# Layer 0's expert blocks 12 to 59: rows turned four at a time by VectorE's square transposes and 16 SBUF transfers, with a lead of eight fetches

## The chip, the cores and the metric

The kernel runs on one core of one Trainium2 chip. The time is that of one execution on the device, in microseconds (us); a comparison uses the median of several runs. A profile is one further execution recorded by the hardware profiler, and takes somewhat longer than the runs without it. PE is TensorE, PEld its weight loads, DVE is VectorE, ACT is ScalarE, POOL is GpSimd, SP is SyncE, whose queue issues most plain DMAs. "L1698" is line 1698 of the kernel before.

## What is computed

Two layers of a transformer-like network on x of shape (4, 1024, 256), each an attention-like part and a mixture of experts, with a layer norm, a modulation and a gate around each. The change concerns the experts of layer 0:

```python
def _L0_ffn_ref(input_emb, W1, b1, W2, b2, Wr, br):
    logits = jnp.einsum('bsd,de->bse', input_emb, Wr) + br
    route_w = jax.nn.softmax(logits, axis=-1)
    _, topk_idx = jax.lax.top_k(route_w, TOP_K)            # 2 of 8 experts
    mask = jax.nn.one_hot(topk_idx, E, dtype=route_w.dtype).sum(-2)
    routed = route_w * mask
    routed = routed / routed.sum(axis=-1, keepdims=True)
    h = jax.nn.relu(jnp.einsum('bsd,edh->ebsh', input_emb, W1) + b1[:, None, None, :])
    expert_out = jnp.einsum('ebsh,ehd->ebsd', h, W2) + b2[:, None, None, :]
    return jnp.einsum('bse,ebsd->bsd', routed, expert_out)
# in reference():
h = _layernorm(x, axis=-1) * (1 + cb) + sb
x = x + gb * _L0_ffn_ref(h, L0_ffn_W1, L0_ffn_b1, L0_ffn_W2, L0_ffn_b2, L0_ffn_Wr, L0_ffn_br)
```

Each expert is a 256 to 1024 to 256 perceptron in fp32. 4096 tokens with two experts each give 8192 pairs of a token and an expert.

## The kernel before

The pairs are sorted by expert into blocks of 128 rows that share one expert, at most 71 blocks. `turning` is 60: blocks 0 to 59 are written out by a hand-ordered loop (L1776 to L1800), and blocks 60 to 67 are placed by a planner together with the start of layer 1 (`late_block`, L1806); the last three run only if the routing needs them. Within `tc.manual_schedule` each engine, SP too, executes its instructions in the order in which the program lists them.

For one block j the work is this.

- `g0.reach` (L746; VectorE, two instructions at L752), `g0.look` (L761; TensorE, two matmuls at L765) and `g0.find` (L774; VectorE) work out which 128 rows of the token table belong to the block. In the loop this is done for block j + 3.
- `g0.fetch` (L791) lets POOL gather these rows, 258 words each (256 features and two that say where the result goes), with an indirect DMA (the helper's line is L347). In the loop it is done for block j + 2, into one of four buffers `xgbuf`.
- `weights_in` and `weights_out` (L1686, L1689) gather W1 (1 MB with its bias) and W2 of the block's expert, double buffered; where the expert is that of two blocks before, the indices point beyond the table and nothing is moved.
- `turn_rows` (L1675) turns the 128 x 256 rows into features on partitions with two TensorE transposes (L1678) into PSUM, and `rows_turned` (L1681) copies them to SBUF on VectorE (L1683).
- `aimed` / `g0.aim` (L1737, L799) computes where the block's results are to be written.
- `hidden` (L1692) is 16 products of W1 with the turned rows, each two matmul instructions (L1698), and `rectified` (L1707) adds the bias and applies the ReLU on ACT (L1710).
- `values` (L1717) is 8 products with W2, again two instructions each (L1721), and `biased` (L1730) adds the second bias on VectorE (L1732); `kept` (L1740) lets POOL write the rows to HBM with a scatter (L812).

Iteration j of the loop lists, for TensorE: hidden of block j, the transposes of block j + 1, the count of block j + 3, values of block j - 1. For VectorE: reach of j + 3, the copy of the turned rows and the address of j + 1, find of j + 3, the bias add of j - 1. For POOL: W1 of j + 1, the scatter of j - 2, W2 of j, the rows of j + 2. `once` (L1765) adds work that belongs to later stages; from iteration 8 to 23 it lists one load of 512 KB each on SP (L1774: the weights and modulations of layer 1).

`early` (L1452) is a pool for tiles of the stage that follows (the combination of the experts' results and layer 1's first norm: `yg1`, `h1`, `hT1` and small ones). W1's rows are laid out on the host so that row p of the gathered tile holds features p and 128 + p, one after the other (L2528).

Of the kernel before, what the change touches and what calls it, by code (L numbers as in the profile page):

```python
# [8 lines left out]
F32 = mybir.dt.float32  # L9
F16 = mybir.dt.float16  # L10
I32 = mybir.dt.int32
# [8 lines left out]
P = 128  # L20
B, S, D = 4, 1024, 256
NC = S // P
KD = D // P
E = 8
H = 1024
KH = H // P
# [6 lines left out]
ROUTER = 64  # L33
STRIP = 32
AHEAD = 3
DX = D + 2
W1ROW = KD * H + KH
W2ROW = KH * D + D
# [101 lines left out]
def adaln_d2_kernel(  # L140
# [20 lines left out]
    nc = tc.nc  # L161
# [8 lines left out]
    ps_m = ctx.enter_context(tc.tile_pool(name="ps_m", bufs=3, space=PSUM))  # L170
# [79 lines left out]
    xgbuf = [pw.tile([P, DX], F32, name=f"xg_{i}") for i in range(4)]  # L250
# [108 lines left out]
    class Pairs:  # L359
# [386 lines left out]
        def reach(self, scratch, j):  # L746

            reached = scratch.tile(
                [P, self.halves, P], F16, tag="g_reached", name="g_reached", bufs=3
            )  # L750
            for h in range(self.halves):
                nc.vector.tensor_scalar(  # L752
                    reached[: self.K, h, :],
                    count16[: self.K],
                    self.limit[: self.K, h, j : j + 1],
                    None,
                    ALU.is_ge,
                )
            return reached
# [35 lines left out]
        def aim(self, scratch, xg, j):  # L795


            dest = scratch.tile([P, 1], I32, tag="g_dest", name="g_dest", bufs=8)
            nc.vector.scalar_tensor_tensor(  # L799
                dest,  # L800
                xg[:, D : D + 1],
                self.code[:, j : j + 1],
                xg[:, D + 1 : D + 2],
                ALU.not_equal,
                ALU.add,
            )
            return dest
# [566 lines left out]
    for piece in range(3):  # L1374
        ps = plan.slot("p2")
        m = loaded
# [72 lines left out]
    mods1 = [l1.tile([P, B, D], F32, name=f"mod{i}") for i in range(6)]  # L1449
    groups = [Pairs(l1, l1, "ga", 4 * B), Pairs(l1, l1, "gb", 3 * B)]  # L1450
    mod_rows1 = dram.tile([B, 6, D], F32, name="mod_rows1")
    early = ctx.enter_context(tc.tile_pool(name="early", bufs=1))  # L1452
    poolF = tc.tile_pool(name="poolF", bufs=2, side="right")
    work = poolF.__enter__()
    y0 = dram.tile([2 * B * S, D], F32, name="y0")
    groups_of["g0"], values_of["g0"] = g0, y0

# [23 lines left out]
    RINGS = tuple(room1)  # L1481
    SP = "SP"
    made = {}
    home = {"yg1": early, "h1": early, "hT1": early, "tiny": early}

    def buf(kind, shape):
        return (home[kind] if kind in home else late).tile(
# [187 lines left out]
    def turn_rows(j):  # L1675
        pt = psum(ps_m, [P, KD, P], "pm_x")
        for k in range(KD):
            nc.tensor.transpose(pt[:, k, :], xgbuf[j % 4][:, k * P : (k + 1) * P], ident)  # L1678
        return pt

    def rows_turned(pt):  # L1681
        xT = work.tile([P, KD, P], F32, tag="xT", name="xT", bufs=3)
        nc.vector.tensor_copy(xT, pt)  # L1683
        return xT

    def weights_in(j):  # L1686
        gather(w1buf[j % 2], W1, g0.wrow[:, j : j + 1], E * P - 1)
# [4 lines left out]
    def hidden(j, xT, m4):  # L1692
        w1 = w1buf[j % 2]
        p1 = psum(ps_1, [P, 4, P], "p1_h")
        for i in range(4):
            m = 4 * m4 + i
            for k in range(KD):
                nc.tensor.matmul(  # L1698
                    p1[:, i, :],
                    lhsT=w1[:, k * H + m * P : k * H + (m + 1) * P],  # L1700
                    rhs=xT[:, k, :],
                    start=(k == 0),
                    stop=(k == KD - 1),
                )
        return p1
# [11 lines left out]
    def values(j, hid):  # L1717
        w2 = w2buf[j % 2]
        p2 = psum(ps_2, [P, D], "p2_y")
        for m in range(KH):  # L1720
            nc.tensor.matmul(  # L1721
                p2,
                lhsT=hid[:, m, :],
                rhs=w2[:, m * D : (m + 1) * D],
                start=(m == 0),
                stop=(m == KH - 1),
            )
        return p2

    def biased(j, p2):  # L1730
        y = work.tile([P, D], F32, tag="y", name="y", bufs=3)
        nc.vector.tensor_tensor(y, p2, w2buf[j % 2][:, KH * D :], ALU.add)  # L1732
        return y

    dests, ys0 = {}, {}

    def aimed(j):  # L1737
        dests[j] = g0.aim(work, xgbuf[j % 4], j)
# [35 lines left out]
            nc.sync.dma_start(*loads[j - 8])  # L1774

    with tc.manual_schedule(engines=ORDERED | {EngineType.SP}):  # L1776
        for j in range(2):
            g0.fetch(xgbuf[j], h_rows, j)
        xT, hid = rows_turned(turn_rows(0)), None
        aimed(0)  # L1780
        for j in range(turning):

            weights_in(j + 1)
            if j > 1:
                kept(j - 2)
            if j:
                weights_out(j)
            g0.fetch(xgbuf[(j + 2) % 4], h_rows, j + 2)
            reached = g0.reach(work, j + AHEAD)
            new = new_hidden()  # L1790
            for m4 in range(2):
                rectified(j, new, hidden(j, xT, m4), m4)

            xT = rows_turned(turn_rows(j + 1))
            aimed(j + 1)
            g0.find(work, g0.look(ps_m, reached), j + AHEAD)
            if j:
                ys0[j - 1] = biased(j - 1, values(j - 1, hid))
            hid = new
            once(j)  # L1800


    plan = Plan(rings=RINGS, **room1)
    of_block = {}

# [762 lines left out]
```

## Time and profile before

| what | value |
|---|---|
| median of three runs (range) | 1121.61 us (1121.43 to 1122.06) |
| the profiled execution | 1141.97 us |
| its span, first to last instruction | 1140.2 us |
| granted TensorE clock, mean | 0.986 |
| blocks 0 to 67 of layer 0's experts, first and last L1698 | 115.0 to 615.1 us of the span |
| L1678, transposes of the rows | 136 instructions, 26.1 us busy |
| L1698, hidden products | 2176 instructions, 254.7 us busy |
| L1721, values products | 1088 instructions, 249.0 us busy |
| L765, counts in this stage | 136 instructions, 19.2 us busy |
| L1683, copies of the turned rows (DVE) | 68 instructions, 28.8 us busy |
| L347, gathers of weights (POOL) | 134 instructions, 135.1 us busy |

A group of the profile gives line, engine, operation, what it writes and reads with the shapes, how often, then busy time, the mean duration of one in ns, the engine's idle time just before the group's instructions and what ended most of it. A line of the timeline gives start and length in us, engine, line, operation and how many instructions were merged, and, in brackets, an idle time before it and what ended it. A line of a window gives its limits, its length, and for PE, PEld, DVE, ACT and POOL the busy time and the number of instructions; then the granted clock, the DMA engines' mean busy share and GB/s.

### The profile page before, as it was taken

Reading aid. Unit: us, or ns where it says so; the run is one execution under the profiler, and the core shown is the slowest. Engines: PE = TensorE matmul, PEld = TensorE weight load, DVE = VectorE, ACT = ScalarE, POOL = GpSimd, SP = SyncE. Lnnn points to the kernel's source line nnn. Section 1 sums busy time; section 2 is a strip of 40 time slices with the busy share of each in tenths; the row PEclk is TensorE's granted clock in tenths of the full one; section 3 lists DMA queues with packets and bytes.
Section 4 is the critical chain, followed back from the end, with each engine's and each line's share of the span. In section 5 each row is a group of like instructions: output and inputs, shape, how many; then the busy total and the mean of one; then the engine's idle time right before and its main releaser. Section 6 shows DMA issues by size and latency. Waiting matters only on the chain. (4 is left out here: it accounts for less than half of the span.)

```text
span 1140.2 us, 18501 instructions
## 1 busy us (share of the span) xinstructions
PE 1086.3 (95%) x6238; PEld 847.0 (74%) x6238; DVE 592.0 (52%) x2308; ACT 428.6 (38%) x1164; POOL 422.5 (37%) x483
## 2 busy tenths in 40 slices
PE   8998999999999999999999999999999999899883
PEld 5894999999999999999988466566576575547641
DVE  7787232222222222222274788975776445888456
ACT  5976333322333323233343343432434235333421
POOL 1000455555555555555543011010044233616452
PEclk8999999999999999999999999999999999999996
DMA  9414549242422415151260312100024223323532
GB/s 321 174 31 103 191 156 302 100 153 75 154 78 75 150 39 192 33 193 40 70 223 27 96 34 83 39 10 19 19 62 129 75 82 103 102 88 107 155 118 93
DMA packets 77693, 122.38 MB, mean 107 GB/s; under 512 B 27340, under 2 KB 57301, under 8 KB 72990
## 3 DMA queue, kind: packets, MB, share of 16 engines
q0 software_dynamic: 31872, 69.68, 19.5%
q1 hardware_dynamic: 44622, 49.92, 13.3%
q10 hardware_dynamic: 1104, 1.58, 0.4%
q8 instruction: 52, 0.85, 0.3%
q14 instruction: 43, 0.35, 0.1%
HBM read 205.25 MB, written 30.22 MB: 207 GB/s over the span
## 5 line engine op out<-in xcount | busy, mean ns | idle before, releaser
L1710 ACT ACTIVATE hid<-p_h,w 128x128 f32<-128x128 f32 x544 | 154.8, 368 | 323.5 <-issue 251.9
L1698 PEld LDWEIGHTS p_h<-xT,w 128*128 128x128 f32 x2176 | 253.2, 192 | 7.2 <-DVE xT L1683 1.9
L1698 PE MATMUL p_h<-xT,w 128*128 128x128 f32 x2176 | 254.7, 275 | 3.1 <-DVE xT L1683 2.7
L1721 PE MATMUL p_y<-w,hid 128*128 128x256 f32 x1088 | 249.0, 382 | 0.2 <-issue 0.2
L2007 PE MATMUL p_u<-hT,a 128*128 128x512 f32 x512 | 232.0, 596 | 2.9 <-ACT hf L2019 1.4
L1721 PEld LDWEIGHTS p_y<-w,hid 128*128 128x128 f32 x1088 | 201.6, 190 | 25.1 <-DMA w<-in_W,g_wrow 0.4
L2007 PEld LDWEIGHTS p_u<-hT,a 128*128 128x128 f32 x512 | 93.5, 190 | 100.5 <-issue 89.7
L347 POOL DMA_INDIRECT w<-in_W,g_wrow x134 | 135.1, 1008 | 77.4 <-ACT hid L1710 46.7
L1683 DVE COPY xT<-pm_x 128x256 f32<-128x256 f32 x68 | 28.8, 424 | 187.0 <-PE pm_x L1678 134.4
L812 POOL DMA_INDIRECT y<-y,g_dest x68 | 69.5, 1022 | 143.5 <-DVE g_reached L752 108.4
L2055 PE MATMUL p_f<-a,hf 128*128 128x256 f32 x512 | 116.7, 380 | 2.0 <-DVE step L2096 1.0
L1732 DVE TENSOR_TENSOR y<-p_y,w 128x256 f32<-128x256 f32 x68 | 28.9, 425 | 166.9 <-PE p_y L1721 160.7
L2055 PEld LDWEIGHTS p_f<-a,hf 128*128 128x128 f32 x512 | 95.9, 190 | 20.8 <-issue 5.9
L347 POOL DMA_INDIRECT xg<-h_rows,g_row x68 | 66.7, 980 | 120.4 <-DVE g_row L787 98.9
L2103 POOL TENSOR_TENSOR x_sb<-x_sb,step 128x256 f32<-128x256 f32 x32 | 24.9, 778 | 205.8 <-DVE step L2096 153.6
L2315 PE MATMUL p_e<-ew,xT 128*128 x280 | 71.5, 386 | 0.8 <-ACT y L2325 0.8
L2019 ACT ACTIVATE hf<-p_u,decay 128x512 f32<-128x512 f32 x56 | 38.2, 685 | 74.9 <-PE p_u L2007 63.5
L347 POOL DMA_INDIRECT xg<-ga_rows,ga_row x39 | 37.3, 956 | 54.1 <-DVE g_hits L778 19.3
L2315 PEld LDWEIGHTS p_e<-ew,xT 128*128 128x128 f32 x280 | 49.0, 190 | 11.0 <-issue 3.8
L2023 DVE SCALAR_TENSOR_TENSOR hf<-p_u,decay,hf 128x512 f32<-128x512 f32 x56 | 41.9, 748 | 25.7 <-PE p_u L2007 14.3
L1618 DVE TENSOR_TENSOR h<-h,mod 128x256 f32<-128x256 f32 x128 | 51.6, 425 | 6.8 <-ACT h L1608 4.1
L2325 ACT COPY y<-p_e 128x256 f32<-128x256 f32 x70 | 26.1, 373 | 51.4 <-PE p_e L2315 19.2
(371 smaller groups left out, 1259.1 us busy)
## 6 DMA issues: line engine op xcount, KB each, us to landing
yg<-y SPq DMA_DIRECT2D x32, 256.0 KB
ga_y<-y SPq DMA_DIRECT2D x39, 128.0 KB
x_sb<-in_x SPq DMA_DIRECT2D x8, 512.0 KB
h_rows<-xn SPq DMA_DIRECT2D x8, 512.0 KB
gb_y<-y SPq DMA_DIRECT2D x31, 128.0 KB
out_x<-x_sb SPq DMA_DIRECT2D x7, 512.0 KB
a<-in_fw SPq DMA_DIRECT2D x6, 512.0 KB
mod<-mod_rows SPq DMA_DIRECT2D x6, 512.0 KB
```

The costliest lines, as they stand in the source:

```text
L347: return nc.gpsimd.indirect_dma_start(out=dst, out_offset=None, in_=table, in_offset=bass.IndirectOffsetOnAxis(ap=index, axis=0), bounds_c ...
L812: nc.gpsimd.indirect_dma_start(out=table, out_offset=bass.IndirectOffsetOnAxis(ap=dest, axis=0), in_=y, in_offset=None, bounds_check=2 * s ...
L1618: nc.vector.tensor_tensor(h, h, mods1[(sc, sh)[i]][:, b, :], (ALU.mult, ALU.add)[i])
L1698: nc.tensor.matmul(p1[:, i, :], lhsT=w1[:, k * H + m * P : k * H + (m + 1) * P], rhs=xT[:, k, :], start=(k == 0), stop=(k == KD - 1),)
L1710: nc.scalar.activation(hid[:, m, :], p1[:, i, :], AF.Relu, bias=w1buf[j % 2][:, KD * H + m : KD * H + m + 1],)
L1721: nc.tensor.matmul(p2, lhsT=hid[:, m, :], rhs=w2[:, m * D : (m + 1) * D], start=(m == 0), stop=(m == KH - 1),)
L1732: nc.vector.tensor_tensor(y, p2, w2buf[j % 2][:, KH * D :], ALU.add)
L2007: nc.tensor.matmul(pu, lhsT=a[:, k, m * P : (m + 1) * P], rhs=made["n1", c, "hT"][:, k, :, :], start=(k == 0), stop=(k == KD - 1),)
L2019: nc.scalar.activation(made[key, m], made[key, m, 0], AF.Silu, scale=decays[c])
L2023: nc.vector.scalar_tensor_tensor(h, made[key, m, 1], decays[c], h, ALU.mult, ALU.mult)
L2055: nc.tensor.matmul(made[key, "p2", b], lhsT=made[key, m][:, b * P : (b + 1) * P], rhs=a1[:, m, :], start=(m == 0), stop=(m == KH - 1),)
L2315: nc.tensor.matmul(made[key, "p2"], lhsT=made[key, "xT"][:, k, :], rhs=ew_flat[:, bass.ds(made[key, "at"] + k * D, D)], start=(k == 0), st ...
```

## The change

Blocks 12 to 59 form twelve groups of four ("quads"). Their rows are gathered into two buffers that hold four blocks each. At the end of iteration j = 8, 12, ..., 52, behind the bias add, `quad_turned` turns the rows of blocks j + 4 to j + 7: for each of the two halves k of the features (every second feature, from k on) one VectorE instruction transposes all 32 x 32 squares of the four blocks, 512 columns on 128 partitions, into `square`. The squares then lie on the wrong partitions, and 16 DMAs from SP's queue, one for each pair of source and destination group of 32 partitions, move them, 1 KB per partition, into the tile `xTq`. The four addresses (`g0.aim`) follow on VectorE. TensorE's transposes and VectorE's copies from PSUM are left out for these 48 blocks; blocks 0 to 11 and 60 on keep them, but read every second feature too, and W1's rows are laid out accordingly on the host (row p holds features 2p and 2p + 1).

`hidden` now reads a half of a quad's block as four runs of 32 words, 1 KB apart. For the longer lead, rows are searched ten blocks ahead and fetched eight blocks ahead: iterations 2 to 8 search two blocks each and 4 to 9 fetch two each; from iteration 53 on nothing is searched and from 54 on nothing is fetched in the loop. The buffers for searches and addresses grow from 3 to 5 and from 8 to 16. The pool `early` is opened only after the loop, on the memory that the quads had.

```diff
--- before.py
+++ after.py
@@ -33,6 +33,8 @@
 ROUTER = 64
 STRIP = 32
 AHEAD = 3
+QUAD = 4
+SQ = 32
 DX = D + 2
 W1ROW = KD * H + KH
 W2ROW = KH * D + D
@@ -746,7 +748,7 @@
         def reach(self, scratch, j):
 
             reached = scratch.tile(
-                [P, self.halves, P], F16, tag="g_reached", name="g_reached", bufs=3
+                [P, self.halves, P], F16, tag="g_reached", name="g_reached", bufs=5
             )
             for h in range(self.halves):
                 nc.vector.tensor_scalar(
@@ -795,7 +797,7 @@
         def aim(self, scratch, xg, j):
 
 
-            dest = scratch.tile([P, 1], I32, tag="g_dest", name="g_dest", bufs=8)
+            dest = scratch.tile([P, 1], I32, tag="g_dest", name="g_dest", bufs=16)
             nc.vector.scalar_tensor_tensor(
                 dest,
                 xg[:, D : D + 1],
@@ -1449,9 +1451,11 @@
     mods1 = [l1.tile([P, B, D], F32, name=f"mod{i}") for i in range(6)]
     groups = [Pairs(l1, l1, "ga", 4 * B), Pairs(l1, l1, "gb", 3 * B)]
     mod_rows1 = dram.tile([B, 6, D], F32, name="mod_rows1")
-    early = ctx.enter_context(tc.tile_pool(name="early", bufs=1))
+    poolQ = tc.tile_pool(name="poolQ", bufs=2)
+    quads = poolQ.__enter__()
     poolF = tc.tile_pool(name="poolF", bufs=2, side="right")
     work = poolF.__enter__()
+    xgquad = [quads.tile([P, QUAD, DX], F32, name=f"xq_{i}", bufs=1) for i in range(2)]
     y0 = dram.tile([2 * B * S, D], F32, name="y0")
     groups_of["g0"], values_of["g0"] = g0, y0
 
@@ -1481,7 +1485,7 @@
     RINGS = tuple(room1)
     SP = "SP"
     made = {}
-    home = {"yg1": early, "h1": early, "hT1": early, "tiny": early}
+    home = {}
 
     def buf(kind, shape):
         return (home[kind] if kind in home else late).tile(
@@ -1675,13 +1679,40 @@
     def turn_rows(j):
         pt = psum(ps_m, [P, KD, P], "pm_x")
         for k in range(KD):
-            nc.tensor.transpose(pt[:, k, :], xgbuf[j % 4][:, k * P : (k + 1) * P], ident)
+            nc.tensor.transpose(pt[:, k, :], xgbuf[j % 4][:, k:D:KD], ident)
         return pt
 
     def rows_turned(pt):
         xT = work.tile([P, KD, P], F32, tag="xT", name="xT", bufs=3)
         nc.vector.tensor_copy(xT, pt)
-        return xT
+        return [xT[:, k, :] for k in range(KD)]
+
+    def in_quads(j):
+        return 3 * QUAD <= j < turning
+
+    def rows_of_block(j):
+        if in_quads(j):
+            return xgquad[j // QUAD % 2][:, j % QUAD, :]
+        return xgbuf[j % 4]
+
+    def quad_turned(j):
+
+        rows = xgquad[j // QUAD % 2]
+        square = quads.tile([P, P // SQ, KD, QUAD, SQ], F32, tag="square", name="square", bufs=1)
+        for k in range(KD):
+            nc.vector.transpose(
+                square[:, :, k, :, :].rearrange("p m b s -> p b m s"),
+                rows[:, :, k:D:KD].rearrange("p b (m f) -> p b m f", f=SQ),
+            )
+        xT = quads.tile([P, P // SQ, KD, QUAD, SQ], F32, tag="xTq", name="xTq")
+        for q in range(P // SQ):
+            for m in range(P // SQ):
+                nc.sync.dma_start(
+                    xT[m * SQ : (m + 1) * SQ, q, :, :, :], square[q * SQ : (q + 1) * SQ, m, :, :, :]
+                )
+        for b in range(QUAD):
+            turned_quads[j + b] = [xT[:, :, k, b, :] for k in range(KD)]
+            dests[j + b] = g0.aim(work, rows[:, b, :], j + b)
 
     def weights_in(j):
         gather(w1buf[j % 2], W1, g0.wrow[:, j : j + 1], E * P - 1)
@@ -1698,7 +1729,7 @@
                 nc.tensor.matmul(
                     p1[:, i, :],
                     lhsT=w1[:, k * H + m * P : k * H + (m + 1) * P],
-                    rhs=xT[:, k, :],
+                    rhs=xT[k],
                     start=(k == 0),
                     stop=(k == KD - 1),
                 )
@@ -1732,7 +1763,7 @@
         nc.vector.tensor_tensor(y, p2, w2buf[j % 2][:, KH * D :], ALU.add)
         return y
 
-    dests, ys0 = {}, {}
+    dests, ys0, turned_quads = {}, {}, {}
 
     def aimed(j):
         dests[j] = g0.aim(work, xgbuf[j % 4], j)
@@ -1774,8 +1805,10 @@
             nc.sync.dma_start(*loads[j - 8])
 
     with tc.manual_schedule(engines=ORDERED | {EngineType.SP}):
+        looks = {0: (3,), 1: (4,)} | {j: (j + 3, j + 10) for j in range(2, 9)}
+        fetches = {j: (j + 2,) for j in range(4)} | {j: (j + 2, j + 8) for j in range(4, 10)}
         for j in range(2):
-            g0.fetch(xgbuf[j], h_rows, j)
+            g0.fetch(rows_of_block(j), h_rows, j)
         xT, hid = rows_turned(turn_rows(0)), None
         aimed(0)
         for j in range(turning):
@@ -1785,21 +1818,33 @@
                 kept(j - 2)
             if j:
                 weights_out(j)
-            g0.fetch(xgbuf[(j + 2) % 4], h_rows, j + 2)
-            reached = g0.reach(work, j + AHEAD)
+            for r in fetches.get(j, (j + 2 * QUAD,)):
+                if r < turning + 2:
+                    g0.fetch(rows_of_block(r), h_rows, r)
+            sought = [r for r in looks.get(j, (j + 2 * QUAD + 2,)) if r < turning + AHEAD]
+            reached = [g0.reach(work, r) for r in sought]
             new = new_hidden()
             for m4 in range(2):
                 rectified(j, new, hidden(j, xT, m4), m4)
 
-            xT = rows_turned(turn_rows(j + 1))
-            aimed(j + 1)
-            g0.find(work, g0.look(ps_m, reached), j + AHEAD)
+            if in_quads(j + 1):
+                xT = turned_quads.pop(j + 1)
+            else:
+                xT = rows_turned(turn_rows(j + 1))
+                aimed(j + 1)
+            for r, hit in zip(sought, reached):
+                g0.find(work, g0.look(ps_m, hit), r)
             if j:
                 ys0[j - 1] = biased(j - 1, values(j - 1, hid))
+            if j % QUAD == 0 and in_quads(j + QUAD):
+                quad_turned(j + QUAD)
             hid = new
             once(j)
 
 
+    poolQ.__exit__(None, None, None)
+    early = ctx.enter_context(tc.tile_pool(name="early", bufs=1))
+    home.update(yg1=early, h1=early, hT1=early, tiny=early)
     plan = Plan(rings=RINGS, **room1)
     of_block = {}
 
@@ -2526,7 +2571,7 @@
         return a.reshape(E, -1, P, a.shape[2]).swapaxes(1, 2).reshape(E, P, -1)
 
     w1 = np.concatenate(
-        [rows(g["L0_ffn_W1"]), g["L0_ffn_b1"].reshape(E, KH, P).swapaxes(1, 2)], 2
+        [g["L0_ffn_W1"].reshape(E, P, -1), g["L0_ffn_b1"].reshape(E, KH, P).swapaxes(1, 2)], 2
     )
     w2 = np.concatenate(
         [
```

## Prediction

> **What bounds the kernel now.** I read the page first (busy shares, groups), then the timeline of one block in the middle of the loop, then the busy time of the whole stretch that the change touches.
>
> ```profile
> span 1140.2 us, 18501 instructions
> PE 1086.3 (95%) x6238; PEld 847.0 (74%) x6238; DVE 592.0 (52%) x2308; ACT 428.6 (38%) x1164; POOL 422.5 (37%) x483
> L1683 DVE COPY xT<-pm_x 128x256 f32<-128x256 f32 x68 | 28.8, 424 | 187.0 <-PE pm_x L1678 134.4
> ```
>
> TensorE is 95% busy; VectorE, which copies the turned rows, mostly waits for TensorE. One block (number 26) in the timeline:
>
> ```profile
> 304.99 3.73 PE L1698 MATMUL p_h<-xT,w 128*128 128x128 f32 x32
> 305.19 0.42 DVE L1732 TENSOR_TENSOR y<-p_y,w 128x256 f32<-128x256 f32 x1 [2.59 <-PE p_y L1721]
> 305.53 0.41 DVE L752 TENSOR_SCALAR g_reached<-count,g_limit 128x128 f16<-128x128 f16 x2
> ...
> 308.56 0.38 PE L1678 MATMUL pm_x<-ident,xg 128*128 128x128 f32 x2
> 308.67 0.21 PEld L765 LDWEIGHTS <-g_reached 128*128 128x128 f16 x2
> ...
> 308.77 0.28 PE L765 MATMUL pm_counts<-g_more,g_reached 128*128 128x129 f16 x2
> ...
> 308.89 3.67 PE L1721 MATMUL p_y<-w,hid 128*128 128x256 f32 x16
> 308.98 0.42 DVE L1683 COPY xT<-pm_x 128x256 f32<-128x256 f32 x1 [3.04 <-PE pm_x L1678]
> 309.32 0.21 DVE L799 SCALAR_TENSOR_TENSOR g_dest<-xg,g_code 128x1 int32<-128x1 f32 x1
> 309.44 0.35 DVE L778 TENSOR_SCALAR_CACHE_REDUCE g_hits<-pm_counts,g_nth 128x128 f16<-128x128 f32 x1
> ...
> 312.40 0.38 PE L1698 MATMUL p_h<-xT,w 128*128 128x128 f32 x2
> ```
>
> The PE lines follow each other without a bracket, that is without idle time: hidden product, two transposes, two matmuls of the count, values, and the next block 7.41 us after the last. Durations contain the pipeline's latency, so I price by starts: hidden 3.57 us, transposes 0.21 (308.56 to 308.77), count 0.12, values 3.51. The stretch of blocks 3 to 59 as a whole:
>
> ```profile
> 127.00:557.00 430.00, 430.00 (x3018) 405.35 (x3017) 104.81 (x477) 133.84 (x466) 231.60 (x231) 1.00 0.38 126
> ```
>
> TensorE (third number) is busy for all of it at the full clock; the block starts in the trace are 7.41 us apart from block 3 to 59 without exception. So TensorE's instruction stream is the bound here, and a piece taken out of it is gained unless something new makes it wait.
>
> [...] The transposes here read every second word, a step [...] no row here shows. [...] the trace has DMAs at a 0.79 share in block 26 and the same 7.41 us. [...]
>
> **Taken out.** For 48 blocks (12 to 59, in iterations 11 to 58) the two L1678 transposes leave TensorE: 48 x 0.214 us = 10.3 us, all of it on the bounding path (bounds 0.15 to 0.27 a block, as neighbours change: late blocks without a count show steps of the same size shift by 0.06). 48 copies of L1683 leave VectorE, worth nothing by themselves.
>
> **Moved.** Searches (L752, L765, L778) and row fetches (L347) keep their number; they run up to seven blocks earlier, two a block in iterations 2 to 8 and 4 to 9. TensorE pays 0.12 us for each extra count then and saves as much in iterations 53 to 59: nothing. POOL issues a second fetch in iterations 4 to 9, 0.98 + 0.30 us; its four instructions take 4.00 of 7.41 us. It delays the next w1 gather by about 0.6 us, which now starts 0.67 us after the fetch ends because it waits for ACT. Cover: by the trace's packets the w1 gather for block 11 lands 3.07 us before use, the later ones in the loop 4.1 to 4.5, the w2 gathers mostly 3.5.
>
> **Added on VectorE.** In each of 12 iterations (8, 12 to 52) two transposes of 512 columns follow the bias add, then four address operations (L799, moved here), and behind them is queued the next block's L752, for which TensorE's count waits. With d for one transpose: L752 ends at 305.53 + 2d + 4 x 0.13 + 0.41, and with about 0.1 us for the semaphore the count can load at 306.56 + 2d. Without the transposes TensorE wants that at 308.67 - 0.21 = 308.46. So the cover is d = 0.95 us. [...]
>
> **Added on SP and the DMA engines.** 16 transfers a group, 32 partitions of 1 KB each. An SP issue took 0.32 us in the median (L1525), so 5.1 us[...], where the first user is hidden three blocks later, at about 326.6. 12 us of cover; if gone, each late us counts once a group. The engines' load: 512 packets, 32 an engine; the 29,952 packets of 1,024 B before took 47 ns in the median, so 1.5 us of all engines per group. Not shown for SBUF to SBUF; twice that still fits.
> The 16 loads of L1774 stood on SP in one burst, 159.7 to 178.6 us, beside no weight gather; now they stand behind the transposes of iterations 8, 12, 16 and 20, four a time (2 MB, some 6 us at the 356 GB/s of 170 to 190 us), and some meet the gathers of blocks 11, 12, 18 and 19 with 3 to 4.5 us of cover against up to 3.6 us of sharing. I take 1 us lost in all, bounds 0 and 4.
>
> **Reads in new shapes.** hidden reads xT in four runs of 128 B in place of one. Two runs against one show no price: p_u (one run) and p_e (two runs) take the same per 44 matmuls,
>
> ```profile
> 630.76 19.15 PE L2007 MATMUL p_u<-hT,a 128*128 128x512 f32 x44 [0.29 <-ACT hf L2019]
> 1088.01 19.05 PE L2363 MATMUL p_e<-ew,hT 128*128 128x512 f32 x44
> ```
>
> so I take nothing; not shown for four. The remaining 20 blocks' transposes load every second word as weights, which no row shows: 40 loads at 0 to 0.11 us (109 ns each doubled), taken as 0.7 us in all, bound 4.4. W1's rows are only permuted; gathers keep 8,224 B a row. The tiles of the next stage now reuse the groups' memory: their first writer, L1525, goes at 571.08, and the last reader, hidden of block 59, is over at 553: 18 us of cover.
>
> **Sum.** 10.3 - 1.0 - 0.7 = 8.6 us. The profiled execution took 1141.97 us (span 1140.2), so 1133.4; the median without profiling is 1121.61, and as the loop waits for nothing but TensorE I carry the same difference over: 1113.0 us.
>
> **Rivals.** (1) Partly given back (0.18): d between 1.0 and 1.25, or gathers of weights arriving late; 4 to 6 us lost again, about 1117.5. For: the one-word step; the cover of 0.95 is near. [...] (2) No change (0.08): [...] 10 us of waits, about 1122. (3) Slower (0.14): [...] then L752 is 2.5 us late in 12 blocks, 30 us lost, 1121.6 + 20 = about 1142. It decides from d = 0.95 + 0.5 x 8.6/12 = 1.3 us on. For: no row of this operation exists. [...]
> (4) That four-run reads slow hidden by a tenth (11 ns x 32 x 48 = 17 us) is inside the slower chance, 0.03 of it.
>
> **How the numbers follow.** Forecast 0.60 (own range 1109.5 to 1116). A measurement of this kernel tells 0.2%, 2.2 us, from no change. Faster: 0.60 + 0.18 = 0.78; same 0.08; slower 0.14. The range from 1109 to 1122.5 takes in the forecast, rival 1 and half of 2, and leaves out the slower case.
>
> **What would show it.** Right: block starts 7.20 us apart in 12 to 59, no PE wait at L765 in iterations 9, 13 to 53[...], xT landing 10 us ahead. Wrong: PE waiting for g_reached once in four blocks (rival 1 to 3, the transposes' duration tells which), PE waiting for w at blocks 11, 12, 18, 19, or hidden's steps above 111 ns.

## The result, and the profile after

| | us |
|---|---|
| before, median of 4 runs (1120.87 to 1122.06) | 1121.52 |
| after, median of 4 runs (1111.16 to 1111.82) | 1111.35 |
| ratio, with its 95% interval | 0.9917 (0.9905 to 0.9929) |
| forecast for after | 1113.0 |
| profiled execution of after, and its span | 1111.26, 1109.5 |

The change makes the kernel 10.2 us (0.8%) faster. The same two kernels side by side a second time (after again, below) gave 0.9927 (0.991 to 0.9944), 7.3 us. From the page of the kernel after come the busy shares and the new transfers (queue, count, size of one):

```profile
span 1109.5 us, 18513 instructions
PE 1067.5 (96%) x6142; PEld 837.6 (75%) x6142; DVE 588.3 (53%) x2284; ACT 429.6 (39%) x1164; POOL 423.3 (38%) x483
xTq<-square SPq DMA_DIRECT2D x192, 32.0 KB
```

TensorE has 96 matmuls fewer, the 48 pairs of transposes. In what follows a group is one of the change's quads of four blocks. In the rows below L1729 is hidden, L1752 values, L1763 the bias add, L1703 the square transpose, L1710 the transfers, L801 the address, L754 the reach, L767 the count, L1682 and L1687 the turning that is left on TensorE and its copy, L349 a gather. The timeline of the kernel after, block 26, which has no square transposes behind it:

```profile
306.27 3.73 PE L1729 MATMUL p_h<-xTq,w 128*128 128x128 f32 x32
306.47 0.42 DVE L1763 TENSOR_TENSOR y<-p_y,w 128x256 f32<-128x256 f32 x1 [2.96 <-PE p_y L1752]
306.81 0.41 DVE L754 TENSOR_SCALAR g_reached<-count,g_limit 128x128 f16<-128x128 f16 x2
...
309.73 0.21 PEld L767 LDWEIGHTS <-g_reached 128*128 128x128 f16 x2
...
309.84 0.28 PE L767 MATMUL pm_counts<-g_more,g_reached 128*128 128x129 f16 x2
...
309.96 3.67 PE L1752 MATMUL p_y<-w,hid 128*128 128x256 f32 x16
```

Between hidden and the count nothing stands any more. The next block starts at 313.47, 7.19 us after this one, where it was 7.41. What TensorE waited for from 115 to 560 us (total in us, times, longest) in the kernel after:

```profile
PE p_y L1752 <- DMA w<-in_W,g_wrow: 2.1, 3, 1.0
PE p_h L1729 <- DVE xT L1687: 1.5, 2, 1.1
PE pm_x L1682 <- DMA xg<-h_rows,g_row: 0.2, 1, 0.2
```

The second line stood in the kernel before too, with the same numbers, at the first blocks. The first is new: three values products wait for gathers of the second weights. Block starts (the first hidden matmul of each block), as differences of before and after in us:

| steps from block to the next | before | after | difference | what it holds |
|---|---|---|---|---|
| 2 to 9 | 59.28 | 60.26 | +0.98 | extra counts of the lead, 0.13 each |
| 11 to 52 | 311.22 | 304.78 | -6.44 | 42 x -0.219, and 2.8 lost in blocks 12 (8.44), 19 (7.73), 20 (8.18) |
| 53 to 58 | 44.46 | 42.20 | -2.26 | 6 x -0.219, and the counts saved again |
| 60 to 66 | 54.54 | 52.54 | -2.00 | block 63 at 8.12, before 9.73 |

Up to block 60, with the steps that the table leaves out, that is 7.9 us, and 2.0 us more in the steps from block 60 to 67, which a planner places.

One remark on the profile of before that stands ahead of the prediction: its execution took 1141.97 us, 20 us over the median of 1121.5. Measured from the first p_u to the end, its last part took 515.19 us; in the kernel after it took 493.54. The runs below show that this difference goes with the chip on which a profile is taken and not with the change. Nor does a profiled execution have to be the longer one: that of the kernel after took 1111.26 us, its median is 1111.35.

### The profile page after: what moved, and what is told of

The parts are those of the page before. It is cut to its first block, busy times and chain, and to the rows that moved or that the text cites. A ratio compares the mean times of both kernels' runs of the same rounds, so it can differ in the third digit from the quotient of the medians.

```text
span 1109.5 us, 18513 instructions
## 1 busy us (share of the span) xinstructions
PE 1067.5 (96%) x6142; PEld 837.6 (75%) x6142; DVE 588.3 (53%) x2284; ACT 429.6 (39%) x1164; POOL 423.3 (38%) x483
## 4 chain that ended last, share of the span: by engine, by line
PE 82%; DVE 8%; DMA 6%; ACT 3%; issue 2%; POOL 0%; SPq 0%; DVEq 0%; ACTq 0%; POOLq 0%
PE p_h L1729 20%; PE p_y L1752 20%; PE p_u L2052 19%; PE p_f L2100 10%; PE p_e L2360 4%; DMA w<-in_W,g_wrow 4%; PE pm_x L2343 1%; PE pm_t L1664 1%; DMA xg<-gb_rows,gb_row 1%; PE pm_counts L767 1%; ACT xn L1004 1%; PE pm_b L1071 1%; PE pm_gram L1130 1%; DVE ln_st L978 1%; ACT h2T L1049 1%
## 5 line engine op out<-in xcount | busy, mean ns | idle before, releaser
L1752 PE MATMUL p_y<-w,hid 128*128 128x256 f32 x1088 | 248.8, 382 | 2.5 <-DMA w<-in_W,g_wrow 2.5
L1752 PEld LDWEIGHTS p_y<-w,hid 128*128 128x128 f32 x1088 | 201.6, 190 | 27.9 <-DMA w<-in_W,g_wrow 3.3
L1729 PEld LDWEIGHTS p_h<-xTq,w 128*128 128x128 f32 x1536 | 179.1, 192 | 2.5
L1729 PE MATMUL p_h<-xTq,w 128*128 128x128 f32 x1536 | 179.2, 275 | 0.0
L349 POOL DMA_INDIRECT w<-in_W,g_wrow x134 | 135.3, 1009 | 77.2 <-ACT hid L1741 47.6
L1763 DVE TENSOR_TENSOR y<-p_y,w 128x256 f32<-128x256 f32 x68 | 28.9, 424 | 212.6 <-PE p_y L1752 192.7
L780 DVE TENSOR_SCALAR_CACHE_REDUCE g_hits<-pm_counts,g_nth 128x128 f16<-128x128 f32 x68 | 23.6, 348 | 104.2 <-PE pm_counts L767 103.1
L1729 PE MATMUL p_h<-xT,w 128*128 128x128 f32 x640 | 75.1, 276 | 1.5 <-DVE xT L1687 1.5
L1729 PEld LDWEIGHTS p_h<-xT,w 128*128 128x128 f32 x640 | 74.1, 192 | 2.5 <-issue 1.2
L349 POOL DMA_INDIRECT xg<-h_rows,g_row x20 | 19.8, 988 | 106.5 <-DVE g_row L789 99.6
L349 POOL DMA_INDIRECT xg<-ga_rows,ga_row x39 | 37.4, 959 | 52.4 <-DVE g_hits L780 17.3
L2360 PEld LDWEIGHTS p_e<-ew,xT 128*128 128x128 f32 x280 | 49.1, 190 | 10.4 <-issue 3.7
```

The lines of the kernel that those rows point to most:

```text
L349: return nc.gpsimd.indirect_dma_start(out=dst, out_offset=None, in_=table, in_offset=bass.IndirectOffsetOnAxis(ap=index, axis=0), bounds_c ...
L1729: nc.tensor.matmul(p1[:, i, :], lhsT=w1[:, k * H + m * P : k * H + (m + 1) * P], rhs=xT[k], start=(k == 0), stop=(k == KD - 1),)
L1752: nc.tensor.matmul(p2, lhsT=hid[:, m, :], rhs=w2[:, m * D : (m + 1) * D], start=(m == 0), stop=(m == KH - 1),)
L2360: nc.tensor.matmul(made[key, "p2"], lhsT=made[key, "xT"][:, k, :], rhs=ew_flat[:, bass.ds(made[key, "at"] + k * D, D)], start=(k == 0), st ...
```

## Experiments

Eleven runs follow, on three chips, numbered 1 to 3 here. Chips differ: before took 1141.78 us on the first, 1142.15 on the second and 1120.79 on the third, so times are compared on one chip only, and across chips only ratios to before. All edits start from the kernel after, except the first. Late blocks are those that took at least 0.25 us more than the blocks beside them.

| chip | run | us | ratio to before (95%) | step, blocks 13 to 52 | block 9 | other late blocks |
|---|---|---|---|---|---|---|
| 1 | before again, one execution | 1144.45 | | 7.413 | 7.41 | none |
| 1 | lead only | 1146.78 | 1.0038 (1.0025 to 1.005) | 7.428 | 7.53 | 6 |
| 1 | both | 1148.0 | 1.0053 (1.0036 to 1.0071) | 7.428 | 10.41 | 11 |
| 1 | loads early | 1135.89 | 0.9942 (0.9924 to 0.996) | 7.194 | 8.26 | 6, 10 |
| 2 | double | 1141.28 | 0.999 (0.9982 to 0.9997) | 7.194, every fourth 7.61 | 9.73 | 11, 12, 20, 49 |
| 2 | double late | 1134.51 | 0.9942 (0.9925 to 0.9958) | 7.194 | 9.19 | 10, 11, 20 |
| 2 | best | 1131.67 | 0.9909 (0.9892 to 0.9925) | 7.194 | 10.15 | none |
| 2 | contig | 1134.97 | 0.9947 (0.993 to 0.9964) | 7.194 | 9.94 | 11, 20 |
| 3 | after again | 1113.45 | 0.9927 (0.991 to 0.9944) | 7.194 | 7.43 | 12, 20, 27 |
| 3 | best again | 1108.42 | 0.9884 (0.987 to 0.9898) | 7.194 | 7.43 | 11 |
| 3 | from 16 | 1108.72 | 0.9886 (0.9872 to 0.99) | 7.194 from 15 on | 7.43 | 19, 27 |

### Before again: where the 20 us of its profile are

> The kernel before, profiled once more. The profiled execution of before took 1141.97 us against a median of 1121.5, that of after 1111.26 against 1111.35. If the 20 us belong to that one execution, this profile's span is near 1120 us and the part after layer 0's experts (from the first p_u on) takes as long as after's, 493.5 us (616.0 to 1109.5); if they belong to the kernel, the span is again near 1140 and that part about 515.

It took 1144.45 us, its last part 514.99 us. The other kernels on chips 1 and 2 have 512 to 517 us there, whatever they change in layer 0; those on chip 3 have 492.7 to 493.6, and the kernel after had 493.54. So the 20 us go with the chip, and lie behind the part that was changed; what differs between the chips was not looked into. The step of the prediction that carried a saving from the long profile over to the median was sound.

### Lead only, and both: the lead is no gain, the turning is

Lead only keeps the lead of eight fetches and the groups' row tiles, but turns every block on TensorE:

```diff
-            if in_quads(j + 1):
-                xT = turned_quads.pop(j + 1)
-            else:
-                xT = rows_turned(turn_rows(j + 1))
-                aimed(j + 1)
+            xT = rows_turned(turn_rows(j + 1))
+            aimed(j + 1)
...
-            if j % QUAD == 0 and in_quads(j + QUAD):
-                quad_turned(j + QUAD)
```

> The change without its turning: rows are searched ten and fetched eight blocks ahead into the two buffers of four blocks, but all are turned on TensorE, block by block, and no square transposes and no transfers are made. If the gain is TensorE's 96 transposes, this is at the time of before, 1121.5 us (block steps 7.41 us in blocks 12 to 59), within 1.5 us. If the longer lead of searches and fetches brings the gain, it is near 1111.

(Aim and the transposes then take the group's row tiles.) It was 0.4% slower than before, 5.0 us in the medians, where at most 1.5 were expected. In the profiles it reaches block 60 only 0.8 us later than before again does (560.27 against 559.47 us), and its last part, which the edit leaves alone, takes 2.2 us more; so most of the 5.0 us is not in the loop, and its cause was not sought. The lead brings no gain. Its steps are 7.428 us in blocks 13 to 52, 0.015 more than before: the transposes that load every second word cost 0.0075 us a load. Blocks 2 to 9 took 1.7 us longer, of which 0.98 are the extra counts and these loads, as in the kernel after. Since nothing on SP waits for VectorE here, its loads run ahead as in before (the six of mod are issued from 164.8 to 173.7 us, in before from 162.8 to 171.5), and blocks 12, 19 and 20 are not late.

Both keeps TensorE's transposes beside the new work. Their results aren't used:

```diff
             if in_quads(j + 1):
                 xT = turned_quads.pop(j + 1)
+                turn_rows(j + 1)
```

> After, with TensorE's two transposes of each of the blocks 12 to 59 made in addition, their result unused. If these transposes cost their issue slots on a full TensorE, block steps go from 7.19 to 7.41 us and the time is 1111.35 + 48 x 0.22 = 1121.9 us. If the transposes were hidden and the gain came from elsewhere, it stays near 1111.4.

Its steps are 7.428 again, with all of the transfers and square transposes in place, so these cost TensorE nothing in an ordinary block. Against the kernel after, the same transfers with 0.234 us of transposes less in a block: 48 x 0.234 = 11.2 us is what taking them off TensorE is worth. The time, 6.2 us over before in the medians where about none was expected, has 3 us from block 9, which is taken up below, and 1.3 from block 11, at whose end hidden of block 12 waits for a gather of weights; block 20 is 0.23 us longer too. Lead only, with the same lead and no transfers, has no such wait: it is the transfers' place on SP that moves the loads. In the kernel after SP issues the first group's transfers from 182.69 to 193.73 us and the first four loads from 193.77 on, the next four from 224.31, then from 253.66 and 282.98; in before all 16 go out from 159.69 to 178.56.

### Loads early: are the late blocks the bunched loads?

```diff
-        if 8 <= j < 8 + len(loads):
-            nc.sync.dma_start(*loads[j - 8])
+        if j == 7:
+            for load in loads:
+                nc.sync.dma_start(*load)
```

> After, with the 16 loads of layer 1's weights and modulations listed in iteration 7, ahead of the first transfers on SP, in place of one each in iterations 8 to 23. If the three long blocks (12, 19, 20; 2.8 us together) come from these loads standing in bunches of four behind the transfers and sharing the DMA engines with the gathers of W2, the long blocks go and the time is 1111.35 - 2.8 = 1108.6 us. If the transfers themselves delay the gathers, they stay and the time is 1111.4.

Blocks 12, 19 and 20 are at 7.19, so these late blocks need the bunched loads. The packets of the gather that brings the second weights for the values product of block 20's step say the same: the last one comes 0.5 to 0.6 us before that product starts in all six profiles with the loads behind the transfers (also in the three that put the wait down to "issue"), and 2.8 us or more before it in loads early, best and best again. In the kernel after, the windows (PE, PEld, DVE, ACT, POOL busy, then the clock, the DMA engines' mean share and GB/s) show the stretch:

```profile
127.00:557.00 430.00, 427.87 (x2974) 402.27 (x2974) 104.20 (x460) 136.10 (x474) 236.54 (x236) 1.00 0.44 141
...
193.00:213.00 20.00, 18.96 (x129) 17.63 (x128) 4.21 (x16) 4.63 (x17) 9.89 (x10) 1.00 0.84 312
202.00:214.00 12.00, 10.96 (x80) 10.26 (x79) 3.79 (x15) 3.02 (x11) 5.57 (x6) 1.00 0.76 295
```

The same 193 to 213 us of before:

```profile
193.00:213.00 20.00, 20.00 (x147) 18.99 (x146) 4.61 (x21) 6.32 (x23) 10.87 (x11) 1.00 0.58 200
```

And the timeline of after, block 12, at the values product that waits:

```profile
207.67 1.56 PE L1752 MATMUL p_y<-w,hid 128*128 128x256 f32 x6 [1.03 <-DMA w<-in_W,g_wrow]
```

With four loads of 512 KB behind the first group's transfers the DMA engines go to a share of 0.84, and TensorE stands still for 1.04 us in that window, nearly all of it for one gather. But the whole did not gain what these blocks lost (ratio 0.9942): blocks 6, 9 and 10 took 0.8, 0.8 and 2.5 us more than they do in the kernel after. That need not be a price of the early loads: with the loads in the same place on chip 3 (best again, from 16) blocks 6 and 9 took their usual 7.55 and 7.43 us and block 10 at most 7.62. Blocks 6 and 10 are of the kind of block 9, below. From this run alone no gain is shown.

The loads aren't all of it either. From 16, described below, has them early, and its values products (L1755 there) waited twice all the same, in blocks 19 and 27:

```profile
PE p_y L1755 <- DMA w<-in_W,g_wrow: 1.1, 2, 0.5
```

In the kernel before, the last packet of these two gathers came 3.6 us before its use; in from 16 it came 0.67 us before it, with a group's transfers beside it and no load; in lead only, which has the lead and no transfers, it was 3.5 us. So the transfers alone can use up a gather's cover. In best and best again the same gathers came 1.0 to 2.4 us ahead, and nothing waited.

### Double and double late: how much cover VectorE had

Double issues each square transpose twice; double late does so too, but puts the group behind the next block's reach:

```diff
-        for k in range(KD):
+        for k in [*range(KD), *range(KD)]:
             nc.vector.transpose(
```

```diff
             reached = [g0.reach(work, r) for r in sought]
+            if j % QUAD == 1 and in_quads(j - 1 + QUAD):
+                quad_turned(j - 1 + QUAD)
...
-            if j % QUAD == 0 and in_quads(j + QUAD):
-                quad_turned(j + QUAD)
```

> After, with each square transpose made twice into the same tile[...]. In after the next block's reach ends at 302.34 and TensorE's count takes it at 302.54 us, so by the cover of the prediction some 0.1 us is left. Then [...] 1.1 us is waited for in each of the twelve, 13.4 us in all: 1124.8 us, and TensorE's counts show waits for g_reached. If VectorE's place doesn't matter, it stays at 1111.4.

> The doubled transposes of the run before, but listed one block later behind that block's reach, so that TensorE's count no longer stands behind them. If the count is what waits, the 13.4 us go again and the time is 1111.4 us within 1.5; if it is the later transfers or a busy VectorE, it stays near 1124.8.

First the timeline of the kernel after, at a group (block 29), with no doubling:

```profile
327.85 3.73 PE L1729 MATMUL p_h<-xTq,w 128*128 128x128 f32 x32
328.05 0.42 DVE L1763 TENSOR_TENSOR y<-p_y,w 128x256 f32<-128x256 f32 x1 [2.96 <-PE p_y L1752]
328.52 1.30 DVE L1703 STREAM_TRANSPOSE square<-xq 128x512 f32<-128x512 f32 x2
...
329.75 0.57 DVE L801 SCALAR_TENSOR_TENSOR g_dest<-xq,g_code 128x1 int32<-128x1 f32 x4
...
330.24 0.41 DVE L754 TENSOR_SCALAR g_reached<-count,g_limit 128x128 f16<-128x128 f16 x2
331.31 0.21 PEld L767 LDWEIGHTS <-g_reached 128*128 128x128 f16 x2
```

Reach ends at 330.65, TensorE loads its result at 331.31 when it has finished hidden, with no wait: 0.66 us are left. The same place in double:

```profile
303.24 3.73 PE L1729 MATMUL p_h<-xTq,w 128*128 128x128 f32 x32
303.44 0.42 DVE L1763 TENSOR_TENSOR y<-p_y,w 128x256 f32<-128x256 f32 x1 [2.41 <-PE p_y L1752]
303.91 2.49 DVE L1703 STREAM_TRANSPOSE square<-xq 128x512 f32<-128x512 f32 x4
...
306.32 0.57 DVE L801 SCALAR_TENSOR_TENSOR g_dest<-xq,g_code 128x1 int32<-128x1 f32 x4
...
306.81 0.41 DVE L754 TENSOR_SCALAR g_reached<-count,g_limit 128x128 f16<-128x128 f16 x2
...
307.11 0.26 PEld L767 LDWEIGHTS <-g_reached 128*128 128x128 f16 x2 [0.33 <-issue]
307.11 0.39 PE L767 MATMUL pm_counts<-g_more,g_reached 128*128 128x129 f16 x2
```

Two transposes more take 2.49 - 1.30 = 1.19 us; blocks with a group then take 7.61 us, 0.415 more and not the 1.1 us expected. So 1.19 - 0.415 = 0.77 us of cover were left over in the kernel after. That VectorE is what is waited for can be read from single instructions: the two reach instructions end at 307.06 and 307.22 us, and each of the count's two loads starts 0.05 us later (307.11 and 307.27); in eight of the ten groups the wait of the count's matmul is put down to g_reached. It follows as well from double late, whose blocks 13 to 52 are all at 7.194, but for 20, with the same four transposes. Its timeline, VectorE only:

```profile
301.80 2.49 DVE L1703 STREAM_TRANSPOSE square<-xq 128x512 f32<-128x512 f32 x4
304.20 0.58 DVE L801 SCALAR_TENSOR_TENSOR g_dest<-xq,g_code 128x1 int32<-128x1 f32 x4
```

The count no longer stands behind them. The pair differs by 6.8 us in the median, 4.2 of which are ten groups at 0.42; the rest is not accounted for.

### Contig: does reading every second word cost VectorE anything?

```diff
-                rows[:, :, k:D:KD].rearrange("p b (m f) -> p b m f", f=SQ),
+                rows[:, :, k * P : (k + 1) * P].rearrange("p b (m f) -> p b m f", f=SQ),
```

(with the transposes left on TensorE and the rows of W1 changed to match, so that the two halves of a row are adjacent features.)

> After, with a half of the features being 128 adjacent ones as in the kernel before, in place of every second one (W1's rows laid out accordingly). If reading every second word costs neither VectorE's transposes nor TensorE's weight loads, it is at 1111.4 us within 1[...]. If the step cost the 20 remaining blocks' weight loads something (prediction: 0.7 us), it is that much faster.

The second transpose of a group starts 0.635 us after the first, as in the kernel after (0.636), and the blocks step by 7.194. Reading in steps of two words is not slower here. As a whole contig was not at the ratio of the kernel after (0.9947 against 0.9917 and 0.9927): its blocks 9, 11 and 20 were late, as in other kernels on this chip. Blocks 3 to 8, but for 7, step by 7.53 instead of 7.55, the price of two strided weight loads seen from the other side.

### Best, best again, after again, from 16: a version that beats both

Best joins two of the edits above: the loads in iteration 7, and the square transposes, single, behind the next block's reach.

> After, with the loads in iteration 7 and the (single) square transposes behind the next block's reach. If the cover in after was just enough, the move alone brings nothing and this is the time of the loads alone, 1108.6 us.

On its chip it had the lowest ratio, 0.9909, though block 9 took 10.15 us. It ran again on chip 3 beside the kernel after.

> All 16 loads behind block 7, and the transposes behind the next block's reach. If this arrangement is better than the changed kernel in truth: 2 to 3 us less than that in the same call, because blocks 12, 19 and 20 no longer wait for gathers (2.8 us), and as many of the 2.6 us of block 9 as the other has. If the bunched loads were only pushed to blocks 6, 9 and 10: within 1 us of it.

> The changed kernel itself, next to kernels that turn the rows in the same way, so that ratios can be compared. If the late block 9 (9 to 10 us in the other kernels with square transposes, where 7.43 is usual) belongs to those variants alone, this one shows 7.43 there and a ratio of 0.991 to 0.993 to the kernel before. If it comes with the chip, or with where the program lies in memory in that execution, this one shows 9 to 10 us in block 9 too and a ratio of 0.994 to 0.996.

Best again took 1108.42 us and after again 1113.45; the intervals of the two ratios do not overlap. The gain of 5.0 us in the medians is more than the 2 to 3 us expected; in the profiles block 20 of after again was at 11.23 us, 3 us more than in the first profile of the same kernel, so what the bunched loads cost varies between executions, and best doesn't have it. With single transposes the kernel after had 0.77 us of cover, so the loads' place is the edit that can be seen to remove a wait; the transposes' place was not tried by itself. What TensorE waited for from 115 to 560 us in best again:

```profile
PE p_h L1729 <- issue: 1.3, 1, 1.3
PE p_h L1729 <- DVE xT L1687: 0.4, 1, 0.4
PE pm_x L1682 <- DMA xg<-h_rows,g_row: 0.3, 1, 0.3
```

No gather of weights is in it. And its window while the loads run:

```profile
160.00:190.00 30.00, 30.00 (x216) 28.31 (x215) 10.97 (x54) 10.64 (x34) 19.94 (x21) 1.00 1.05 350
```

The DMA engines are full for 30 us and TensorE never stops. The 1.3 us at p_h is block 12's hidden: the first group's last transfer landed at 202.50 us, 0.58 us before that hidden began at 203.08, where the second group has 7.3 us. The bracket names no releaser, so that the late transfers are the cause is read from these two times; from 16, which has no transfers there, has no such wait.

Block 9 was late (9.2 to 10.4 us) in five kernels on chips 1 and 2, with a wait put down to "issue". Windows of best:

```profile
185.00:190.00 5.00, 3.49 (x15) 2.36 (x16) 0.62 (x3) 0.88 (x4) 1.91 (x2) 1.00 1.07 350
```

and of after:

```profile
185.00:190.00 5.00, 5.00 (x33) 4.61 (x32) 1.46 (x8) 0.64 (x3) 3.13 (x4) 1.00 0.57 148
```

From 16 was to tell whether this comes from the first group's transfers. It is best with the first group turned on TensorE:

```diff
-            if in_quads(j + 1):
+            if by_squares(j + 1):
...
-            if j % QUAD == 1 and in_quads(j - 1 + QUAD):
+            if j % QUAD == 1 and by_squares(j - 1 + QUAD):
```

(by_squares begins at block 16; below that the group's rows are turned on TensorE.)

> As the run beside it with the loads behind block 7, but blocks 12 to 15 turned on TensorE again, so the first square transposes and their 16 transfers come at block 13 instead of block 9; 4 x 0.22 = 0.9 us more for certain. If the late block 9 is TensorE's fetch of instructions held up by the first group's transfers (they start at 183.8 us, the fetch that is usually seen at 185.6 is seen at 190.6): block 9 is back at 7.4 to 7.6 and, with no fetch near the next group's start, no other block is late; 1 to 2 us less than the run beside it. If it comes with the first use of that part of the program: a late block of 9 to 10 us at 13 instead. If it has nothing to do with the transfers: block 9 stays at 9 to 10 us and the whole is 0.9 us longer.

It doesn't decide it: block 9 was at 7.43 us on this chip in after again and best again too. Its four blocks on TensorE stepped by 7.43, 0.9 us in all as expected, yet the time is that of best again (0.9886 against 0.9884): it lacks the late block 11 (8.72 us in best again) and has 0.75 us more in each of 19 and 27, the two gathers shown above.

What can be said of block 9: it goes with the chip as well as with the kernel. Best took 10.15 us there on chip 2, and 7.43 on chip 3. And it isn't TensorE's stream alone that is late. In best ScalarE does all of the block's activations at once ("remote" stands for a releaser that the profile does not name):

```profile
189.12 2.17 ACT L1741 ACTIVATE hid<-p_h,w 128x128 f32<-128x128 f32 x8 [10.74 <-remote]
```

That is 8.1 us after the block's first hidden product, though TensorE's records have hidden at its usual pace. In the five late blocks it is 7.6 to 8.6 us, and 7.1 in block 10 of loads early; in the profiles of before and after and the three of chip 3 it is 2.03 us in every block from 2 to 58. So what ScalarE waits for from TensorE came late there, and the records of TensorE don't tell why. In these five kernels, too, a packet of 16 KB on the instruction queue is recorded 8.6 to 9.8 us after the block's start; in the other eight traces it is 4.8 to 8.4 us after it (loads early, late at 9 and 10 in its own way, among them). In best TensorE is back at its pace at 189.0 us and the packet is recorded at 190.6, so it may as well be late because TensorE was late. The cause stays open.

## Why the prediction was right, step by step

The forecast was 1113.0 us, a saving of 8.6; measured were 10.2 us, and 7.3 on chip 3. The mechanism is the one forecast: TensorE is the bound, and its transposes are gained. That the sum came out so near is in part luck, as its last lines below say.

- **Taken out, 48 x 0.214 = 10.3 us.** Steps show 0.219 a block, 10.5 us. Bounds were 0.15 to 0.27.
- **Moved: nothing.** Right as a sum: 0.98 us more in steps 2 to 9, and 2.26 - 6 x 0.219 = 0.95 us less in 53 to 58.
- **VectorE, cover d = 0.95 us, nothing lost.** Right. That d would stay within its cover was the author's estimate: no row of before shows this transpose, nor a step of two words. The groups of VectorE in the kernel after:

```profile
L1703 DVE STREAM_TRANSPOSE square<-xq 128x512 f32<-128x512 f32 x24 | 15.7, 690 | 0.9 <-issue 0.4
```

  By double, whose further transposes start 0.593 us after one another, that is what a transpose adds. The one step of before that comes near is the bias add's: 256 columns, and the next instruction 0.34 us later (305.19 to 305.53). Twice that, 0.68 us, is an estimate for 512 columns, and the transposes were under it. Reading every second word did not slow them (contig: 0.635 us from the first to the second, the kernel after 0.636). For the semaphore the forecast took about 0.1 us; in double the loads start 0.05 us after the reach instructions end. The cover worked out, 2 x 0.95 us, less 2 x 0.593, leaves 0.71 us; measured 0.77. Rivals 2 and 3, and the first half of rival 1, rested on d above 1.0, which was not shown either, and fall by that number; double shows that this wait was real and would have begun at d of about 0.98. The second half of rival 1, gathers of weights arriving late, came true in part: see the loads.
- **SP, 16 x 0.32 = 5.1 us of issues, 12 us of cover.** Mis-sized. All transfers of the kernel after (minimum, median, maximum in ns):

```profile
L1710 SPq DMA_DIRECT2D xTq<-square x192: 507/589/1742, 182.7 to 512.4; - x192
```

  At 589 ns and some 44 ns between, 16 issues take 10 us (10.3 to 11.6 from first to last in the trace), and the last packet landed 7.5 to 8.0 us before its first use in eight of the twelve groups, 4.8 and 5.7 in two where it met gathers (their packets have a share of 0.99 and 0.86 of the DMA engines in the second us behind the issues, in the eight others 0 to 0.49); the two groups with loads of the same packet size behind them can't be read so. The cover held, so the error cost nothing. Packets took 46 to 53 ns in the median of a group, against 47 taken. The time for landing in the forecast's cover was the author's estimate, shown by no row of before; here, on SP's queue, the last packet came 1.0 to 1.5 us after the last issue had ended in those eight groups.
- **Loads behind the transposes, 1 us (0 to 4).** The place was right, blocks 12, 19 and 20, and the mechanism was shown by loads early. The size was off: 2.8 us, inside the bounds; after again lost 5.1 in its blocks 12 and 20, outside them. TensorE waiting for w was one of the signs named for being wrong. The forecast also put the transfers' own share in the gathers' delay at nothing; from 16 shows two waits of 0.53 us without the loads.
- **Four-run reads of hidden: nothing.** Right: hidden's steps are 111 to 112 ns in both kernels.
- **Strided weight loads of the other 20 blocks, 0.7 us (at most 4.4).** Measured 0.015 us a block by lead only and by contig, 0.3 us.
- **Early pool, 18 us of cover.** The first transfer into the reused memory was issued at 562.5 us, hidden of block 59 ended at about 546.4: 16 us, no wait.

With the measured sizes the sum is 10.5 - 2.8 - 0.3 = 7.4 us, and 7.9 us were seen up to block 60. What the forecast did not have are the 2.0 us of steps 60 to 66. In the four traces that turn all blocks on TensorE, block 63 took 9.2 to 10.6 us; in the nine with turning by squares 7.4 to 9.4. In before it begins at 579.93 us, among the next stage's reads of yg (issued from 571.1 us on) and the last gathers of weights (up to 614.0), and TensorE's longest wait up to the next block is 1.2 us, for the copy of the turned rows, with 0.2 us for a gather; in the kernel after it waits 0.4 us, for a gather. Why it waits less was not tried. Best had 7.43 us there and best again, the same kernel, 9.12; so it isn't shown that these 2.0 us of one pair of profiles come from the change. Without them the saving is the 7.4 to 7.9 us of the loop, near the 7.3 of chip 3.

## What to carry to other kernels

Where one engine's stream is the bound, as TensorE's was here (busy for all 430.00 us of the loop in before), look for work that another engine can do inside its own slack: the transposes were gained at the full step, 0.22 us a block. What decided was not the mean load of the second engine (VectorE 52 to 53% busy) but which of its later instructions the bound engine waits for, so put the new work behind that one (double late against double: 7.194 against 7.61 us in blocks with a group). When a new issue that waits is placed on a DMA queue, look at everything listed behind it on that queue: here the loads that had been free came 34 us later (193.77 us, before 159.69) and in bunches of four, and cost 2.8 us or more. Count, too, what new transfers take from the cover of the old ones: a gather that came 3.6 us ahead came 0.7 us ahead beside them. Moving those loads ahead of the new issues and the transposes behind the reach gave 1108.4 us, 5 us under the changed kernel on the same chip.

## What the runs showed of the hardware that was not expected

- VectorE's 32x32 transposes of 4-byte words, 512 columns each, were as fast from every second word as from adjacent words: starts 0.636 us apart in the kernel after, 0.635 in contig. From every second word, further ones start 0.593 us after one another (double).
- An SP issue of an SBUF to SBUF transfer of 32 rows of 1 KB took 589 ns in the median; the 256 KB loads of yg on the same queue took 320 ns (median) in the same trace.
- The first transpose of a group that reuses the buffers starts 0.47 us after the bias add, the first group's 0.34: 0.13 us, with ten semaphores recorded in its wait in place of two. One group in each of six traces took 0.82 us.
- Weight loads in steps of two words cost about 7.5 ns each on a step of 109 (lead only: 7.428 us a block with two such loads, before again 7.413).
